# Stacking both heads of a pair on the partitions, with the odd heads' half-chunks swapped, in the state-space stage of a decoder layer

## The chip, the cores and the metric

The kernel runs on one core of one Trainium2 chip. The metric is the device time of one execution in microseconds. Everything is fp32.

## The reference

The input is x of 4 x 1024 tokens of width 256, with 16 heads of 16 channels. A layer applies three blocks, each followed by a residual addition and a layer norm: a state-space block (mamba2 with 64 states), cross-attention to 77 context tokens, and a feed-forward block with 1024 hidden units. The change concerns the first block:

```python
logA = einsum(W_logA, x) + b_logA                  # one decay per token and head
XBC  = silu(einsum(W_XBC, x) + b_XBC)              # per head: X 16, B 64, C 64
cum  = cumsum(logA over tokens)
A    = exp(cum_i - cum_j) for j <= i, else 0
G    = einsum('bihn,bjhn->bhij', C, B)
Y    = einsum('bhij,bjhc->bihc', A * G, X)
x    = layernorm(x + (gate(x) * Y) @ W_out.T + b_out)
```

## The kernel before

The 4096 tokens are cut into 16 units of 256 tokens; `stage_a`, `stage_b` and `stage_c` do the three blocks of a unit. In `stage_a` a unit has two chunks of 128 tokens (`chunk_a`), and a chunk has two half-chunks, q = 0 and 1, of L = 64 tokens. Within a half-chunk Y is computed directly through G; what comes from earlier tokens goes through a state of 64 x 16 per head, carried from one half-chunk to the next.

No scheduler reorders the work. Each step is a `part` with a name, and the tables `WHEN` and `EDGE` give each a due time in units, relative to its own unit; all parts are sorted by due time and issued in that order. The table therefore fixes the order on every engine and every queue, and lets three or four units overlap. PSUM has eight banks, handed out by one pool in that same order. All loads go through SyncE's queue, apart from the first weights, which go through ScalarE's.

The parts of the first block, with the line of their main operation:

- `pl` (L594), `cum` (L602): decay logits and their cumulative sum, written to DRAM twice by `cd` (L609) and `ce` (L614). `dl` (L622) reads `cd` back, each half-chunk's rows spread over 64 partitions; `ec` (L631) does so with `ce`, with channels on the partitions. `pcum` and `ncum` (L643, L651) give the negated sums with tokens on the partitions.
- `pb` (L674): B and C of eight heads in four banks. The rows of `bct` hold the 64 states of an even head over the 64 of an odd one. `th` (L686) and `bct` (L694) apply the silu.
- `px`, `zx`, `thx`, `xz` (L739 to L761): X with tokens on the partitions. `xz` is padded with zeros, so that the two heads of a pair write disjoint channels.
- `ex` (L798) and `sel` (L807): the decay matrix, made in place in `dl`, eight heads at a time, and its causal mask.
- `de`, `dex`, `xw` (L772 to L785): X weighted by the decay to the end of the half-chunk.
- `ptb` (L816) and `bk` (L821): B turned so that tokens are on the partitions, for four pairs at a time.
- `pg` (L834) and `st` (L845): G for each head and half-chunk on a 64x64 tile of the array, multiplied into `dl`.
- `pc`, `sn`, `pts`, `new` (L858 to L890): a half-chunk's contribution to the states, the new states with channels on the partitions (`stateT`), and those turned (`state`).
- `pyo` (L908) and `py` (L923): the output from the old states and the output within the half-chunk. `ya`, `yg`, `po_a` (L935 to L951) join them, apply the gate and project.

Before the change the rows of a tile are the 128 tokens of a chunk. A product over one half-chunk therefore runs on 64 of the 128 rows, once for each head of a pair:

```python
lhsT=xz[js, half, 4 * k + r, :],
rhs=s[f"dl{c}"][js, k, 2 * r + half, :],
start=(half == 0), stop=(half == 1),
```

In `pc` the 32 channels of a pair meet the 128 states of both heads, and half of what is made (one head's channels by the other head's states) is not used.

Of the kernel before, what the change touches and what calls it, by code (L numbers as in the profile page):

```python
# [20 lines left out]
P = 128  # L21
# [3 lines left out]
L = 64  # L25
# [12 lines left out]
    "s_c": -17.7488, "s_x": -14.3181, "s_g": -10.9930, "s_b": -8.9191, "s_x2": -8.5921,  # L38
    "keys": -6.9902, "values0": -5.1040, "s_bc": -4.2504, "s_l": -3.8501, "keys0": -3.5178,
    "load_u": -3.5043, "pl": -3.0616, "cum": -3.0081, "s_q": -2.8763, "s_z": -2.8594,  # L40
    "cd": -2.7014, "pcum": -2.4443, "ncum": -2.4136, "load_t": -2.3861, "load_u1": -2.3655,
    "dl0": -2.2598, "keys1": -2.2466, "values1": -2.2259, "px0": -2.1743, "zx0": -2.1414,
    "thx0": -1.9640, "load_k": -1.9383, "pgt": -1.9261, "px1": -1.9192, "gT": -1.8781,
    "ce": -1.8740, "zx1": -1.7566, "de0": -1.7390, "thx1": -1.5753, "ec": -1.4244,
    "ex00": -1.4225, "dex0": -1.4038, "pb0": -1.3989, "th00": -1.3867, "xz0": -1.3838,
    "bct00": -1.3681, "ex01": -1.3369, "th01": -1.3079, "load_k0": -1.3045, "dl1": -1.2878,
    "bct01": -1.2542, "sel00": -1.2073, "xw0": -1.2015, "xz1": -1.1765, "values2": -1.0810,
    "pb1": -1.0622, "de1": -1.0216, "th10": -1.0177, "bct10": -0.9976, "th11": -0.9410,
    "bct11": -0.9385, "dex1": -0.9338, "ptb00": -0.9194, "bk00": -0.8852, "ptb10": -0.8540,
    "ecx": -0.8381, "sel01": -0.8288, "values3": -0.8153, "ptb01": -0.7975, "bk01": -0.7706,  # L50
    "ex11": -0.7660, "pg0": -0.7380, "pc0": -0.7363, "bk10": -0.7222, "xb": -0.6773,
    "sn0": -0.6753, "ptb11": -0.6360, "xw1": -0.6250, "bk11": -0.6233, "st0": -0.5947,
    "sel11": -0.5768, "pts0": -0.5684, "new0": -0.5621, "s_o": -0.5243, "pc1": -0.5148,
    "py0": -0.5044, "ex10": -0.4941, "pyo0": -0.4936, "sn1": -0.4930, "ya0": -0.4577,
    "pg1": -0.4242, "sel10": -0.4139, "yg0": -0.4116, "st1": -0.3962, "pts1": -0.3944,
    "new1": -0.3793, "py1": -0.3293, "pyo1": -0.3263, "ya1": -0.2759, "poa0": -0.1943,
    "yg1": -0.1933, "r10": -0.1344, "poa1": -0.1251, "mv_a0": -0.1056, "r11": -0.0850,
    "mv_a1": -0.0791, "rs_a0": -0.0707, "ln_a0": -0.0569, "rs_a1": 0.0238, "ln_a1": 0.0482,
    "pt_b0": 0.1070, "pt_b1": 0.1865, "xT_b": 0.2141, "pq": 0.2890, "q": 0.3115, "pm1": 0.4314,
    "mx1": 0.4558, "pm0": 0.5218, "mx0": 0.5433, "s_p": 0.6203, "x1b": 0.6256, "pmt": 0.6521,  # L60
    "qm0": 0.6802, "s_1": 0.6869, "qm1": 0.7177, "pe0": 0.7713, "es01": 0.7828, "es00": 0.7874,
    "pe1": 0.8410, "s_2": 0.8624, "es11": 0.8703, "es10": 0.9335, "pa0": 0.9380, "pa1": 0.9881,
    "ot1": 1.0166, "om1": 1.0905, "ot0": 1.1466, "o1": 1.1757, "om0": 1.1997, "o0": 1.2276,
    "pob0": 1.3446, "r20": 1.4077, "pob1": 1.4668, "r21": 1.4989, "mv_b0": 1.5448,
    "mv_b1": 1.6506, "rs_b1": 1.6768, "rs_b0": 1.8518, "ln_b1": 1.8927, "ln_b0": 1.8942,
    "pt_c0": 2.2380, "pt_c1": 2.2437, "xT_c": 2.2515, "x2b": 2.2926, "ph0": 2.5349, "h0": 2.6045,
    "ph2": 2.6287, "h2": 2.6610, "ph3": 2.7023, "h3": 2.7622, "ph1": 2.8178, "h1": 2.8490,
    "pf00": 2.9287, "pf01": 3.0566, "pf10": 3.1025, "r30": 3.2254, "pf11": 3.2529, "r31": 3.2586,
    "mv_c0": 3.3511, "rs_c0": 3.6688, "ln_c0": 3.7881, "mv_c1": 3.9591, "rs_c1": 4.7458,
    "out0": 4.9977, "ln_c1": 5.5578, "out1": 6.9616,  # L70
# [4 lines left out]
        "pl": -3.6206, "cum": -3.5601, "pb0": -3.0592, "cd": -2.9747, "th00": -2.8248,  # L75
        "dl0": -2.7065, "px0": -2.6887, "pgt": -2.5368, "zx0": -2.4855, "pcum": -2.4453,
        "bct00": -2.3636, "th01": -2.2306, "gT": -2.2275, "px1": -2.1555, "zx1": -2.1167,
        "ce": -2.0684, "pb1": -2.0435, "ncum": -2.0328, "dl1": -1.9370, "thx0": -1.7699,
        "de0": -1.7454, "thx1": -1.6968, "xz0": -1.6803, "bct01": -1.6554, "ex01": -1.5524,
        "th10": -1.4592, "ec": -1.4554, "ex00": -1.4510, "ptb00": -1.4249, "sel00": -1.4027,  # L80
        "bct10": -1.3567, "bk00": -1.3010, "de1": -1.2646, "ptb10": -1.2606, "sel01": -1.1913,
        "dex0": -1.1695, "xw0": -1.1362, "th11": -1.1294, "ex11": -1.1040, "bct11": -1.0825,
        "ptb01": -1.0550, "ecx": -1.0519, "ptb11": -0.9216, "dex1": -0.8815, "xz1": -0.8643,
        "xw1": -0.8293, "bk01": -0.8006, "pc0": -0.7667, "ex10": -0.7473, "pg0": -0.7364,
        "bk10": -0.6954, "sel11": -0.6914, "sn0": -0.6792, "pts0": -0.6740, "bk11": -0.6307,
        "st0": -0.6270, "pg1": -0.6051, "new0": -0.5845, "sel10": -0.5719, "pc1": -0.5356,
        "st1": -0.5245, "pyo0": -0.5012, "sn1": -0.4950, "py0": -0.4915, "ya0": -0.4733,
        "yg0": -0.4595, "pts1": -0.4067, "xb": -0.3770, "new1": -0.3550, "py1": -0.3456,
        "pyo1": -0.3330, "ya1": -0.2992, "poa0": -0.2319, "r10": -0.2065, "yg1": -0.1630,
        "poa1": -0.1066, "mv_a0": -0.0350, "r11": -0.0322, "rs_a0": -0.0267, "mv_a1": -0.0199,  # L90
        "ln_a0": 0.0194, "rs_a1": 0.0479, "ln_a1": 0.1008, "pt_b0": 0.1064, "pt_b1": 0.1429,
        "xT_b": 0.2244, "pq": 0.2319, "q": 0.3225, "pm1": 0.4306, "mx1": 0.4701, "pm0": 0.5743,
        "mx0": 0.5866, "pmt": 0.6101, "qm0": 0.6234, "qm1": 0.6498, "pe0": 0.6979, "es00": 0.7094,
        "pe1": 0.8329, "es01": 0.8584, "es10": 0.8642, "pa0": 0.9414, "es11": 0.9582,
        "pa1": 0.9886, "ot1": 1.0223, "om1": 1.0444, "ot0": 1.1639, "om0": 1.2555, "o0": 1.2718,
        "o1": 1.2842, "x1b": 1.2969, "pob0": 1.3403, "r20": 1.4155, "mv_b0": 1.4607,
        "rs_b0": 1.4846, "pob1": 1.6460, "r21": 1.6872, "mv_b1": 1.8206, "rs_b1": 1.8604,
        "ln_b1": 1.9000, "ln_b0": 1.9037, "pt_c1": 1.9838, "pt_c0": 2.0646, "xT_c": 2.2368,
        "x2b": 2.5250, "ph0": 2.5464, "h0": 2.5900, "ph2": 2.6457, "h2": 2.6550, "ph1": 2.6766,
        "h1": 2.7411, "ph3": 2.7854, "h3": 2.8515, "pf00": 2.9091, "pf01": 3.0321, "pf10": 3.0347,  # L100
        "r30": 3.0595, "mv_c0": 3.1626, "pf11": 3.2205, "r31": 3.2894, "rs_c0": 4.4879,
        "mv_c1": 4.9536, "ln_c0": 5.6343, "rs_c1": 5.7231, "ln_c1": 6.4175, "out1": 6.9249,
        "out0": 7.0749,
    },
    1: {
        "pl": -3.0129, "pgt": -2.9113, "load_t": -2.8785, "cum": -2.6494, "cd": -2.6211,
        "pcum": -2.5596, "ncum": -2.2968, "px0": -2.2290, "dl0": -2.1919, "dl1": -1.8956,
        "zx0": -1.8203, "de0": -1.6453, "gT": -1.5667, "ex00": -1.5550, "thx0": -1.5525,
        "pb0": -1.4885, "th00": -1.4645, "xz0": -1.3885, "bct00": -1.3615, "dex0": -1.3462,
        "de1": -1.3143, "pb1": -1.2968, "th01": -1.2908, "ce": -1.2696, "load_k": -1.2501,  # L110
        "bct01": -1.2328, "px1": -1.2052, "ec": -1.1819, "zx1": -1.1474, "sel00": -1.1469,
        "xw0": -1.1209, "ex10": -1.1165, "th10": -1.1064, "ptb00": -1.0814, "ex01": -1.0691,
        "bk00": -1.0479, "ptb10": -1.0460, "bct10": -1.0155, "dex1": -1.0119, "th11": -0.9797,
        "thx1": -0.9660, "bct11": -0.8922, "sel01": -0.8844, "ex11": -0.8518, "pg0": -0.8321,
        "ptb01": -0.8265, "bk01": -0.7690, "xz1": -0.7583, "st0": -0.7572, "pc0": -0.6996,
        "sel10": -0.6991, "ecx": -0.6912, "sn0": -0.6839, "ptb11": -0.6648, "bk10": -0.6566,
        "bk11": -0.5382, "xb": -0.5286, "xw1": -0.5093, "pts0": -0.5046, "pc1": -0.4985,
        "py0": -0.4934, "sn1": -0.4909, "new0": -0.4804, "pyo0": -0.4450, "ya0": -0.4443,
        "pg1": -0.4252, "sel11": -0.4000, "pts1": -0.3929, "st1": -0.3926, "new1": -0.3821,
        "py1": -0.3595, "yg0": -0.3463, "pyo1": -0.3094, "ya1": -0.3049, "poa0": -0.2638,  # L120
# [50 lines left out]
def decoder_layer_kernel(ctx: ExitStack, tc: tile.TileContext, a: dict, out: bass.AP):  # L171
# [21 lines left out]
    def bank(shape, name):  # L193
        return ps.tile(shape, F32, tag="bank", name=name)
# [1081 lines left out]
```

## Time and profile before

| | us |
|---|---|
| median of 3 runs | 709.96 (708.72 to 715.87) |
| the profiled execution | 708.51 |
| its span, from the first to the last instruction | 706.8 |
| TensorE busy | 665.4 |
| TensorE weight loads, overlapping it | 524.1 |
| VectorE busy | 515.3 |
| ScalarE busy | 403.4 |
| GpSimd busy | 296.0 |

PE is TensorE's matmuls and PEld its weight loads; DVE is VectorE, ACT ScalarE, POOL GpSimd, and SP SyncE, which issues most transfers. The timeline gives the start and length of a burst, the engine, the line, the tiles (written <- read), and for a product the tile of the array (rows * columns) and the shape that streams through it, then the number of records. The ends of matmuls are modelled, so the printed length of a burst reaches into the next. An idle engine that is not the bottleneck costs nothing.

### The profile page before, as it was taken

The page shows a single profiled execution, that of the slowest core. Times are in us where ns is not written, and L with a number is a line of the kernel's source. Part 1 is how long each engine was busy: PE and PEld are TensorE (multiplying, and loading weights), DVE is VectorE, ACT ScalarE, POOL GpSimd, SP SyncE. Part 2 cuts the span into 40 slices and gives each one's busy share as a digit, 9 for nine tenths or more (in the row PEclk, how much of TensorE's full clock was granted, in tenths as well). Part 3 has the DMA queues.
Part 4 walks back from the last instruction along what each step waited for, and adds up shares of the span by engine and source line. Part 5 has one row for each costly group of instructions (what it writes and reads, how often), then busy time and mean ns, then how long its engine had stood idle before and what let it go on. Part 6 is the DMA issues. An engine that isn't in the chain of part 4 may idle for free.

```text
span 706.8 us, 26495 instructions
## 1 busy us (share of the span) xinstructions
PE 665.4 (94%) x11088; PEld 524.1 (74%) x11088; DVE 515.3 (73%) x1402; ACT 403.4 (57%) x1107; POOL 296.0 (42%) x525
## 2 busy tenths in 40 slices
PE   1768979999999999999999999999999999999996
PEld 0446757778878787877878787877878787777785
DVE  2636969986878778787877778686887778766643
ACT  0257768865647666575655666575666657631300
POOL 2423525544325445453444345453444435442322
PEclk9969999999999999999999999999999999999999
DMA  4543563222103022322203022222203200000001
GB/s 118 120 119 106 148 166 114 73 56 66 61 26 102 4 71 62 78 80 59 76 26 110 10 78 64 78 80 63 64 17 92 80 1 19 2 17 2 16 15 45
DMA packets 38547, 45.67 MB, mean 65 GB/s; under 512 B 10320, under 2 KB 33565, under 8 KB 38429
## 3 DMA queue, kind: packets, MB, share of 16 engines
q1 hardware_dynamic: 36960, 43.58, 21.9%
q8 instruction: 88, 1.44, 0.8%
q10 hardware_dynamic: 1468, 0.41, 0.3%
q14 instruction: 31, 0.25, 0.1%
HBM read 38.73 MB, written 5.24 MB: 62 GB/s over the span
## 4 chain that ended last, share of the span: by engine, by line
PE 90%; DMA 4%; issue 2%; DVE 1%; POOL 1%; SPq 0%; POOLq 0%; ACT 0%; ACTq 0%
PE ph L1144 16%; PE pf L1171 16%; PE pg L834 5%; PE po_a L951 5%; PE pe L1053 5%; PE pb L674 5%; PE pq L981 4%; PE pa L1078 4%; PE ptb L816 4%; PE po_b L1114 4%; PE py L923 3%; PE pm L1006 3%; DMA xu<-in_xT_dram 3%; PE pc L858 3%; PE py L908 2%; PE pts L881 2%
## 5 line engine op out<-in xcount | busy, mean ns | idle before, releaser
L798 ACT ACTIVATE dl<-dl,ncum 128x64 f32<-128x64 f32 x512 | 127.6, 337 | 0.4
L1144 PE MATMUL ph<-T_c,w 128*128 128x256 f32 x512 | 122.5, 385 | 0.0
L1171 PE MATMUL pf<-w,hT 128*128 128x256 f32 x512 | 120.8, 382 | 0.0
L807 POOL TENSOR_SCALAR_AFFINE_SELECT dl<-dl 64x512 f32<-64x512 f32 x128 | 83.9, 655 | 83.7 <-ACT dl L798 79.4
L1171 PEld LDWEIGHTS pf<-w,hT 128*128 128x128 f32 x512 | 94.2, 190 | 17.1 <-issue 5.4
L1144 PEld LDWEIGHTS ph<-T_c,w 128*128 128x128 f32 x512 | 93.8, 190 | 15.2 <-issue 2.0
L1064 ACT ACTIVATE es<-pe,mb 77x512 f32<-77x512 f32 x128 | 77.0, 680 | 46.8 <-PE pe L1053 46.8
L686 ACT ACTIVATE th<-pb 128x512 f32<-128x512 f32 x128 | 70.9, 594 | 53.4 <-PE pb L674 44.7
L694 DVE SCALAR_TENSOR_TENSOR bct<-th,pb 128x512 f32<-128x512 f32 x128 | 81.6, 679 | 8.2 <-ACT th L686 7.8
L821 ACT COPY bk<-ptb 128x512 f32<-128x512 f32 x64 | 37.2, 585 | 67.7 <-PE ptb L816 55.2
L1017 DVE TENSOR_REDUCE maxes<-pm 128x4 f32<-128x308 f32 x128 | 52.1, 470 | 9.1 <-PE pm L1006 9.1
L1160 ACT ACTIVATE hT<-ph,b 128x256 f32<-128x256 f32 x64 | 26.8, 472 | 51.8 <-PE ph L1144 36.5
L1096 POOL TENSOR_TENSOR on<-at,rec 128x256 f32<-128x256 f32 x32 | 20.2, 632 | 72.3 <-DVE rec L1091 72.3
L1155 DVE TENSOR_SCALAR hT<-ph,b 128x256 f32<-128x256 f32 x64 | 27.9, 478 | 28.0 <-PE ph L1144 28.0
L674 PE MATMUL pb<-xt,w_bc 17*64 17x256 f32 x1024 | 40.7, 396 | 4.9 <-DVE vz L506 1.8
L845 DVE TENSOR_TENSOR dl<-pg,dl 128x512 f32<-128x512 f32 x64 | 40.9, 680 | 6.1 <-PE pg L834 5.1
L548 POOL TENSOR_SCALAR rs_a<-mv_a 128x1 f32<-128x1 f32 x32 | 8.9, 277 | 75.0 <-DVE mv_a L543 73.6
L871 DVE SCALAR_TENSOR_TENSOR stateT<-stateT,ec,pc 128x128 f32<-128x128 f32 x112 | 31.8, 341 | 11.2 <-PE pc L858 9.0
L816 PE MATMUL ptb<-ident,bct 128*128 128x128 f32 x256 | 39.8, 283 | 0.0
L834 PE MATMUL pg<-bct 64*64 64x64 f32 x2048 | 38.0, 221 | 1.5 <-issue 1.4
L834 PEld LDWEIGHTS pg<-bct 64*64 64x64 f32 x2048 | 33.3, 134 | 7.7 <-issue 6.6
L951 PE MATMUL po_a<-w_out,yg 128*128 128x256 f32 x128 | 37.2, 415 | 0.0
(125 smaller groups left out, 1250.1 us busy)
## 6 DMA issues: line engine op xcount, KB each, us to landing
dl<-cd SPq DMA_DIRECT2D x64, 256.0 KB
xt<-in_xT_dram SPq DMA_DIRECT2D x64, 64.0 KB
xu<-in_xT_dram SPq DMA_DIRECT2D x16, 256.0 KB
ec<-ce SPq DMA_DIRECT2D x32, 128.0 KB
xk<-in_x_dram SPq DMA_DIRECT2D x16, 256.0 KB
out_dram<-r SPq DMA_DIRECT2D x32, 128.0 KB
w<-in_w_dram SPq DMA_DIRECT2D x2, 1024.0 KB
kv_w<-in_k_w_dram SPq DMA_DIRECT2D x1, 512.0 KB
```

What stands on the lines that cost most here:

```text
L674: nc.tensor.matmul(pbs[r][64 * half : 64 * half + 64, bc, :], lhsT=w_bc[rs, 2 * gk + half, bc, :], rhs=xt[rs, 2 * gk + half, :], start=Tru ...
L686: nc.scalar.activation(th, s[f"pb{gk}"][r], AF.Tanh)
L694: nc.vector.scalar_tensor_tensor(t, s[f"th{gk}{r}"], 1.0, s[f"pb{gk}"][r], ALU.add, ALU.mult)
L798: nc.scalar.activation(dl[:, k, h, :], dl[:, k, h, :], AF.Exp, bias=s["ncum"][:, c, 8 * k + h : 8 * k + h + 1],)
L807: nc.gpsimd.affine_select(out=d, in_=d, compare_op=ALU.is_ge, fill=0.0, base=0, pattern=[[0, 8], [1, L]], channel_multiplier=-1,)
L816: nc.tensor.transpose(v[f"ptb{k}"][:, r, :], s["bct"][4 * k + r][:, 0, cs], ident)
L834: nc.tensor.matmul(pgs[a][L * q : L * q + L, k, r, :], lhsT=t[64 * a : 64 * a + 64, 0, ts], rhs=t[64 * a : 64 * a + 64, 1, ts], start=True ...
L951: nc.tensor.matmul(v["po"], lhsT=v["yg"][:, k, :], rhs=w_out[:, k, :], start=(k == 0), stop=(k == 1),)
L1017: nc.vector.tensor_reduce(mx[:, :, at : at + 2], s[f"pm{c}"][r].rearrange("p k a s -> p a k s"), AX.X, ALU.max, negate=True,)
L1064: nc.scalar.activation(e, s[f"pe{gp}"][r], AF.Exp, bias=mb[:, b : b + 1], scale=CH**-0.5)
L1144: nc.tensor.matmul(ph[:, j, :], lhsT=w1[:, k, f * P : (f + 1) * P], rhs=s["xT"][:, k, :], start=(k == 0), stop=(k == 1),)
L1171: nc.tensor.matmul(pf, lhsT=s["hT"][:, f, c * P : (c + 1) * P], rhs=w2[:, f, :], start=(f == 0), stop=(f == FF // P - 1),)
```

## The change

The rows of a tile are no longer the 128 tokens of a chunk. For each half-chunk q the rows 0 to 63 and 64 to 127 hold the same 64 tokens for the two heads of a pair: for q = 0 the even head comes first, for q = 1 the odd head (`half ^ q` in the code). The even heads' tokens then stand in the order of the chunk, and the odd heads' half-chunks are exchanged. It follows:

- `py` is one product per pair and half-chunk over all 128 rows, and no longer two on 64 rows; so is `pc`, whose second operand is 64 wide. `stateT` is half as wide.
- `pg` makes the same products, but a bank holds one q and both row tiles of the array write to it, on different halves of its partitions.
- B is turned by halves: `ptb` makes sixteen transposes of 64 rows per chunk instead of eight of 128, into one bank per head of the pair. `bk` becomes four copies of 64 rows per chunk instead of two of 128, and has one buffer instead of two. So has `xw`, which is made in one operation on twice the elements.
- To put the tokens in place, `px`, `pts` and `pcum` are cut into products 32 columns wide. `pts` is an ordinary product with the identity now, and no transpose. `pb` writes B of the odd heads with the half-chunks exchanged, in two products of 128 columns. `xz` is written in four pieces of 64 rows instead of two of 128.
- `dl` is loaded by four transfers per chunk of half the size, instead of two. `b_l`, `w_l` and `b_x` get a second arrangement in the setup, with two more loads for `b_l` and two more for `b_x`.
- `ya` covers both half-chunks in one operation (`py` is one bank). `WHEN` and `EDGE` are replaced as a whole, so the order of all work is another. SyncE's first transfers were xu of unit 0, b_g (8 of them), cd, q_w, q_b, dl of chunk 0, xu of unit 1, ce, dl of chunk 1; they are now xu of units 0 and 1, b_g, cd, ce, cd of unit 1, dl of both chunks, xu of unit 2.

The core of the diff:

```diff
@@ dl
-                    nc.sync.dma_start(
-                        out=dl[L * q : L * q + L].rearrange("p k h i -> p (k h) i"),
-                        in_=s["cd"][2 * c + q, 0:16].partition_broadcast(L),
-                    )
+                    for half in range(2):
+                        a8 = 8 * (half ^ q)
+                        nc.sync.dma_start(
+                            out=dl[L * half : L * half + L, q],
+                            in_=s["cd"][2 * c + q, a8 : a8 + 8].partition_broadcast(L),
+                        )
@@ pb
+                for bc, half, q in ((0, 0, None), (0, 1, 0), (0, 1, 1), (1, 0, None), (1, 1, None)):
...
+                            o = o.rearrange("n (c q i) -> n q c i", c=NC, q=2)[:, 1 - q]
+                            i = i.rearrange("n (c q i) -> n q c i", c=NC, q=2)[:, q]
@@ px
-                nc.tensor.matmul(
-                    v["px"][:, :, k, :], lhsT=xus[u][:, k, cs],
-                    rhs=w_x[:, k].rearrange("x a c -> x (a c)"), start=True, stop=True,
-                )
+                for q in range(2):
+                    for m in range(4):
+                        at = c * P + L * q + 32 * (m % 2)
+                        nc.tensor.matmul(
+                            v["px"][32 * m : 32 * m + 32, q, k, :],
+                            lhsT=xus[u][:, k, at : at + 32],
+                            rhs=w_x[:, k, m // 2 ^ q, :], start=True, stop=True,
+                        )
@@ xz
+                for q in range(2):
+                    nc.vector.scalar_tensor_tensor(
+                        xz[js, q, :, half ^ q, :], thx[:, q], 1.0, zx[:, q], ALU.add, ALU.mult
+                    )
@@ xw
+            v["xw"] = tile_([P, 2, H // 2, 2 * CH], "xw", f"xw_{n}", bufs=1)
@@ ptb, bk
-                for r in range(4):
-                    nc.tensor.transpose(v[f"ptb{k}"][:, r, :], s["bct"][4 * k + r][:, 0, cs], ident)
-                v[f"bk{k}"] = tile_([P, 4, P], "bk", f"bk_{n}_{k}")
-                nc.scalar.copy(v[f"bk{k}"], v[f"ptb{k}"])
+            v["ptb"] = [bank([P, H // 2, NS], f"ptb_{n}_{a}") for a in range(2)]
+            for pair in range(H // 2):
+                for a in range(2):
+                    rs = slice(64 * a, 64 * a + 64)
+                    nc.tensor.transpose(
+                        v["ptb"][a][:, pair, :], s["bct"][pair][rs, 0, cs], ident[rs, rs]
+                    )
...
+                bk = once(v, "bk", lambda: tile_([P, 2, H // 2, NS], "bk", f"bk_{n}", bufs=1))
+                for half in range(2):
+                    js = slice(64 * half, 64 * half + 64)
+                    nc.scalar.copy(bk[js, half ^ a], v["ptb"][a][js])
@@ pg
-                                pgs[a][L * q : L * q + L, k, r, :],
+                        ns, to = slice(64 * a, 64 * a + 64), a ^ q
+                            pgs[q][64 * to : 64 * to + 64, h, :],
@@ pc
+                            v["pc"][32 * r : 32 * r + 32, q, k, :],
+                            lhsT=v["xw"][:, q, 4 * k + r, :], rhs=v["bk"][:, q, 4 * k + r, :],
@@ pts
-                    nc.tensor.transpose(
-                        v["pts"][:, q, k].rearrange("n r a c -> n (r a c)"), sn[:, q, k, :], ident
-                    )
+                    for m in range(4):
+                        nc.tensor.matmul(
+                            v["pts"][32 * m : 32 * m + 32, q, k],
+                            lhsT=sn[:, q, k, 32 * (m % 2) : 32 * (m % 2) + 32],
+                            rhs=ones[:, m // 2], start=True, stop=True,
+                        )
@@ py
-                                lhsT=xz[js, half, 4 * k + r, :],
-                                rhs=s[f"dl{c}"][js, k, 2 * r + half, :],
-                                start=(half == 0), stop=(half == 1),
+                            lhsT=xz[:, q, 4 * k + r].rearrange("p a c -> p (a c)"),
+                            rhs=s[f"dl{c}"][:, q, 4 * k + r, :], start=True, stop=True,
```

## The prediction

> **What bounds the kernel now.** I read the totals first, then a table by stage, then the chain of work that ended last, and then single stretches of the timeline.
>
> ```profile
> PE 665.4 (94%) x11088; PEld 524.1 (74%) x11088; DVE 515.3 (73%) x1402; ACT 403.4 (57%) x1107; POOL 296.0 (42%) x525
> ```
>
> TensorE (PE) is busy 94% of the span. Where are the other 6%? The table by stage (from:to, length, then the busy us of PE, weight loads, VectorE, ScalarE, GpSimd, granted clock, DMA share, GB/s):
>
> ```profile
> 0.00:20.00 20.00, 2.04 (x8) 0.95 (x12) 4.01 (x17) 1.28 (x1) 5.50 (x17) 1.00 0.42 108
> 20.00:54.00 34.00, 24.71 (x264) 16.48 (x268) 18.49 (x51) 16.11 (x52) 10.75 (x23) 0.80 0.51 125
> 54.00:74.00 20.00, 16.88 (x422) 12.67 (x412) 14.32 (x42) 15.12 (x47) 8.98 (x16) 0.91 0.41 114
> 74.00:110.00 36.00, 31.04 (x737) 23.55 (x738) 29.66 (x79) 25.77 (x71) 15.22 (x25) 0.95 0.57 153
> ...
> 200.00:300.00 100.00, 99.99 (x1681) 79.46 (x1673) 78.14 (x215) 61.63 (x166) 44.96 (x78) 1.00 0.22 60
> 300.00:400.00 100.00, 100.00 (x1799) 79.37 (x1795) 78.38 (x213) 63.90 (x181) 44.65 (x79) 1.00 0.22 63
> ```
>
> From 110 us on TensorE never stops. All its idle time lies in the first 110 us (18.0 + 9.3 + 3.1 + 5.0 = 35.4 us) and in the 5 us after its last product. So beyond the head one thing counts: TensorE's own time per unit. In the head two waits for a unit's transposed input carry the chain:
>
> ```profile
> 24.41 12.31 DMA xu<-in_xT_dram
> 38.27 10.37 DMA xu<-in_xT_dram
> ```
>
> **Prices.** In a stretch without idle, a burst costs the start of the next burst minus its own start; the printed length of a burst overlaps the next.
>
> ```profile
> 306.16 1.16 PE L834 MATMUL pg<-bct 64*64 64x64 f32 x64
> 307.25 1.22 PE L674 MATMUL pb<-xt,w_bc 17*64 17x256 f32 x32
> ...
> 310.93 0.86 PE L923 MATMUL py<-dl,xz 64*32 64x64 f32 x64
> 311.72 0.65 PE L908 MATMUL py<-bct,state 128*32 128x64 f32 x32
> 312.31 1.99 PE L1144 MATMUL ph<-T_c,w 128*128 128x256 f32 x8
> ...
> 324.25 0.41 PE L594 MATMUL pl<-xu,w_l 128*32 128x64 f32 x16
> 324.48 1.05 PE L1078 MATMUL pa<-es,vz 77*32 77x256 f32 x16
> ...
> 328.15 0.60 PE L816 MATMUL ptb<-ident,bct 128*128 128x128 f32 x4
> 328.59 0.61 PE L739 MATMUL px<-w_x,xu 128*128 128x128 f32 x4
> 329.04 1.89 PE L1171 MATMUL pf<-w,hT 128*128 128x256 f32 x8
> ```
>
> Three things are read here. (1) A transpose is one record, any other product two: ptb has 256 records for 256 transposes, px 128 for 64 products. (2) Small products on different tiles of the array run side by side: pl, 32 columns wide, is 16 records in 324.48 - 324.25 = 0.23 us, 14 ns each, where four tiles share a stream of some 57 ns. (3) A burst followed by another tile shape pays an exit: the 32 records of L908 should be 32 x 14 = 0.46 us and take 0.59 before ph, so about 0.12; by the same reckoning pg (16 steps of 58 ns = 0.93, takes 1.09) pays 0.16, py 0.14, a full 128x128 burst 0.09.
>
> **Part by part, TensorE per chunk (32 chunks).**
> ptb: eight transposes of 128 rows, 8 x 0.109 = 0.87 us, become sixteen of 64 rows, in two row tiles and two banks, with half as many moving columns. No row shows a 64x128 tile. From above: no overlap of the two row tiles, 16 x 58 ns = 0.93 us, no gain. From below: full overlap, 0.47 us. The nearest row, pg with 64-row tiles, overlaps fully, so I take 0.50: -0.37 a chunk, -11.9 us. [...]
> py: 64 records on 64-row tiles (0.79 less exit 0.14 = 0.65 us) become 32 on full rows, 32 x 14.5 = 0.47: -5.9 us.
> px, pts: full-width products of 0.45 and 0.47 us become 32 narrow records of 0.47 each: +0.8 us. pc: 0.46 to 0.47, nothing. [...] pcum: 4 records to 16: +0.9 us over 16 units. pb: 32 records to 40; a tile's stream is the same, two halves of 128 for one of 256; one step more per half tile, 0.03 us, +0.9 us.
> Sum of streams: -11.9 - 5.9 + 0.8 + 0.9 + 0.9 and +0.3 for pc = **-14.9 us**.
> Exits: px, pts, pc, py and pyo now share one shape (128 rows by 32 columns), while ptb gets a shape of its own. Counted along both programs' order of products there are 371 changes of shape before and 337 after; with the exits above 47.8 us becomes 43.8, **-4.0 us**.
> TensorE in all: -19 us. About 2.5 of 16 units do their part in the starved head, where it saves nothing: -3 back. **-16.**
>
> **The other engines, all under TensorE's cover.** ScalarE: bk turns from one copy of 128 rows into two of 64 rows; the time goes with the elements of a row (585 ns for 512), so 64 more copies, +37 us. VectorE: xz in 128 pieces instead of 64 (303 ns, same length), +19; stateT half as wide (from 341 to about 285), -6; ya joined, -9; de, -3; about zero. GpSimd: xw in one 128x512 operation at 1.27 us (the row of x1b) for two of 0.40, +16. Per 100 us ScalarE goes from 62 to about 71, VectorE stays near 80, GpSimd near 48; none is the bound. SyncE issues 64 more transfers of half the size, at 0.5 us each on a queue that has room; the bytes are the same. If bk's cover went, the whole +37 would come on top.
> **What bk's cover is.** bk and xw lose their second buffer. bk of chunk 1 waits for pc of chunk 0, and pc of chunk 1 for bk. In units 2 to 13 TensorE does between the two pc at least half a feed-forward product (1.73), pg (1.09), and pts (0.47), about 3.5 us; ScalarE needs four copies at about 0.55 from start to start and dex, 2.5 us. It fits. I take 1 us of small waits in all.
> **The head.** Every place in the order changes. xu of unit 1 is now asked for right behind that of unit 0, ahead of eight b_g transfers, so the first wait goes. But xu of unit 2 still follows ce (3.75 us of issue) and two sets of dl, and pl of unit 2 stands ahead of pb1 of unit 0 on TensorE; ptb now needs all eight bct. By that order pg of the first chunk, at 53.2 us now, comes at 50 to 54. Four more small loads (b_l, b_x) stand in ScalarE's queue, 0.7 us each, beside the wait for xu at 19.9. Bounds -8 and +8, since the two waits shown are 22 us and half the idle is spread; I take -2, as one wait goes and the next moves up little.
> Sum: 708.5 (profiled execution) - 16 + 1 - 2 = 691.5. The median shown, 709.96, lies 1.4 above that execution; I say **692**.
>
> **Rivals.**
> A. The transposes don't gain: loads bind or row tiles don't overlap. Then 12 us come back: 704. [...]
> B (slower). ScalarE comes late for bk in each chunk. The cover is 3.5 us, the chain 2.5; one group of eight exponentials of dl in between is 2.0 us (2.01 at 311.33 in ScalarE's timeline), and TensorE would wait 1.0 us a chunk: 691.5 + 32 = 724. It decides from 0.5 us a chunk. For it: one buffer, and ScalarE at 71%. Against it: nearly all of ScalarE's idle time ended with a TensorE result, so it has been early, and no exponentials stand between the pc in units 2 to 13.
> [...]
> D. The head loses the second input wait too, 10.4 us: 681.
>
> **Numbers.** Forecast (684 to 700) 0.55, A with half-gains 0.18, B 0.11, C 0.07, D 0.05, anything else 0.04. A measurement here can tell about 1%, 7 us, from no change. Faster by that: the forecast, D and a third of A, 0.66; same: the rest of A, 0.12; slower: B, C and the rest, 0.22. The range of 8 in 10 runs from 680, most of D, to 724, which takes in A and about half of B and C; the likeliest case's own is 684 to 700.
>
> **What would show it.** Right: TensorE still at 100% in the middle windows; a ptb burst of 16 in about 0.5 to 0.65 us; py in 0.47; pg still 1.09; ScalarE near 440 us busy. Wrong: a ptb burst over 0.85 (A), TensorE idle before pc ended by bk (B), pg near 2 us (C). I am wrong altogether if TensorE is not full after 110 us for another reason, such as VectorE's sn or xz late for pts and py.

## The result: no gain, and the profile after

The changed kernel takes 709.47 us (705.49 to 712.31, 20 runs), the kernel before, on the same chip, 710.93 (20 runs): a ratio of 0.9974, with a 95% interval of 0.9951 to 0.9996. The forecast was 692 us. The profiled execution of the changed kernel took 709.57 us, 1.1 more than that of before.

First the totals of the profile after:

```profile
PE 655.3 (93%) x12504; PEld 513.8 (73%) x12504; DVE 530.1 (75%) x1382; ACT 442.2 (62%) x1171; POOL 308.5 (44%) x493
```

TensorE's busy time fell by 10.1 us (665.4 before), yet the span grew from 706.8 to 707.8, so its idle time grew by 11.1. The table by stage shows where (columns as in the prediction):

```profile
0.00:20.00 20.00, 4.92 (x27) 2.58 (x28) 4.15 (x20) 0.01 (x1) 4.93 (x15) 1.00 0.39 108
20.00:54.00 34.00, 20.16 (x401) 14.58 (x394) 21.96 (x53) 16.52 (x51) 8.20 (x18) 0.85 0.39 114
54.00:74.00 20.00, 15.74 (x495) 12.08 (x492) 13.90 (x41) 14.98 (x40) 9.90 (x15) 0.83 0.35 97
74.00:110.00 36.00, 31.99 (x847) 23.42 (x849) 28.02 (x72) 34.02 (x97) 19.91 (x30) 1.00 0.58 168
...
300.00:400.00 100.00, 98.99 (x2037) 78.88 (x2028) 81.67 (x217) 69.69 (x191) 47.04 (x72) 1.00 0.21 64
```

In the head, the first 110 us, TensorE idles 15.1 + 13.8 + 4.3 + 4.0 = 37.2 us, 1.8 more than before. The rest is new: from 110 to 600 us it is busy 479.9 of 490 us, against 489.4 before. The list of TensorE's waits between 110 and 660 us (total, times, longest) held one wait of 0.6 us before and sums to 9.9 us now. Its three largest entries after:

```profile
PE py L941 <- issue: 4.4, 6, 1.0
PE py L954 <- issue: 2.0, 2, 1.7
PE pm L1035 <- issue: 1.4, 1, 1.4
```

"issue" means that the profile shows nothing the product waited for: no tile, no other engine.

Now the bursts. Two stretches of TensorE's timeline after (start, length, burst); as in the prediction, a burst costs the next start minus its own:

```profile
311.24 1.35 PE L696 MATMUL pb<-xt,w_bc 17*64 17x256 f32 x40
312.52 0.65 PE L941 MATMUL py<-bct,state 128*32 128x64 f32 x32
312.99 0.63 PE L954 MATMUL py<-dl,xz 128*32 128x64 f32 x32
...
334.89 1.22 PE L843 MATMUL ptb<-ident,bct 64*128 64x64 f32 x32
336.04 1.99 PE L1010 MATMUL pq<-T_b,q_w 128*128 128x256 f32 x8
337.97 1.16 PE L866 MATMUL pg<-bct 64*64 64x64 f32 x64
339.06 0.65 PE L887 MATMUL pc<-bk,xw 128*32 128x64 f32 x32
```

The small transposes came out as forecast: the 32 of a burst, for two chunks, cost 336.04 - 334.89 = 1.15 us, exit included. So did py, 0.47 us for 32 records, and pg still costs 1.09. But pb costs 312.52 - 311.24 = 1.28 us, where the shortest gap to the next burst before was 322.31 to 323.36, 1.05.

Last, the waits. This stretch shows what "issue" looks like in the timeline; the bracket is idle time ahead of a burst:

```profile
225.09 0.65 PE L954 MATMUL py<-dl,xz 128*32 128x64 f32 x32
225.56 0.63 PE L912 MATMUL pts<-ident,stateT 128*32 128x64 f32 x32
226.01 0.62 PE L941 MATMUL py<-bct,state 128*32 128x64 f32 x30
227.22 0.27 PE L941 MATMUL py<-bct,state 128*32 128x64 f32 x2 [0.59 <-issue]
```

The halt stands in the middle of a burst: 30 records go, and the last two, of the same tiles, come 0.59 us later. Late data is a poor reason for that. Most of these halts lie in py, pts and pm, behind some 200 to 260 records in 6 us, and each one of more than 0.6 us ends 2.2 to 2.8 us after the start of a packet on q8, the queue that the profile calls "instruction".

### The profile page after: what moved, and what is told of

Same layout as the page of the kernel before. It is cut to its first block, busy times and chain, and to the rows that moved or that the text cites. A ratio compares the mean times of both kernels' runs of the same rounds, so it can differ in the third digit from the quotient of the medians.

```text
span 707.8 us, 29317 instructions
## 1 busy us (share of the span) xinstructions
PE 655.3 (93%) x12504; PEld 513.8 (73%) x12504; DVE 530.1 (75%) x1382; ACT 442.2 (62%) x1171; POOL 308.5 (44%) x493
## 4 chain that ended last, share of the span: by engine, by line
PE 82%; ACT 6%; DMA 3%; issue 3%; DVE 2%; SPq 2%; POOL 1%; ACTq 1%; POOLq 0%; DVEq 0%
PE ph L1173 16%; PE pf L1200 16%; PE pb L696 5%; PE pe L1082 4%; PE po_b L1143 4%; PE po_a L980 4%; PE pg L866 4%; PE pa L1107 4%; PE pq L1010 3%; PE pm L1035 3%; PE py L941 2%; ACT dl L822 2%; PE py L954 2%; PE ptb L843 2%; ACT bk L854 2%
## 5 line engine op out<-in xcount | busy, mean ns | idle before, releaser
L1200 PE MATMUL pf<-w,hT 128*128 128x256 f32 x512 | 122.5, 384 | 0.0
L1173 PEld LDWEIGHTS ph<-T_c,w 128*128 128x128 f32 x512 | 93.8, 190 | 18.1 <-DVE r L988 3.4
L854 ACT COPY bk<-ptb 64x512 f32<-64x512 f32 x128 | 74.2, 579 | 42.6 <-PE ptb L843 38.7
L831 POOL TENSOR_SCALAR_AFFINE_SELECT dl<-dl 64x512 f32<-64x512 f32 x128 | 86.9, 679 | 18.8 <-ACT dl L822 13.8
L974 POOL TENSOR_TENSOR yg<-ya,gT 128x256 f32<-128x256 f32 x32 | 23.4, 730 | 134.0 <-DVE ya L969 134.0
L1125 POOL TENSOR_TENSOR on<-at,rec 128x256 f32<-128x256 f32 x32 | 19.9, 621 | 90.6 <-DVE rec L1120 87.9
L809 POOL TENSOR_TENSOR xw<-xz,de 128x512 f32<-128x512 f32 x32 | 33.6, 1048 | 33.0 <-PE pc L887 27.8
L696 PE MATMUL pb<-xt,w_bc 17*64 17x256 f32 (+1 forms) x1280 | 45.2, 354 | 1.3 <-issue 1.3
L1184 DVE TENSOR_SCALAR hT<-ph,b 128x256 f32<-128x256 f32 x64 | 27.8, 477 | 13.9 <-PE ph L1173 13.8
L696 PEld LDWEIGHTS pb<-xt,w_bc 17*64 17x64 f32 x1280 | 29.2, 135 | 12.4 <-ACT es L1093 4.4
L790 DVE SCALAR_TENSOR_TENSOR xz<-thx,zx 64x128 f32<-64x128 f32 x128 | 37.8, 333 | 0.4
```

The source lines that it names most:

```text
L696: nc.tensor.matmul(o, lhsT=w_bc[rs, 2 * gk + half, bc, :], rhs=i, start=True, stop=True)
L831: nc.gpsimd.affine_select(out=d, in_=d, compare_op=ALU.is_ge, fill=0.0, base=0, pattern=[[0, 8], [1, L]], channel_multiplier=-1,)
L854: nc.scalar.copy(bk[js, half ^ a], v["ptb"][a][js])
L1173: nc.tensor.matmul(ph[:, j, :], lhsT=w1[:, k, f * P : (f + 1) * P], rhs=s["xT"][:, k, :], start=(k == 0), stop=(k == 1),)
L1200: nc.tensor.matmul(pf, lhsT=s["hT"][:, f, c * P : (c + 1) * P], rhs=w2[:, f, :], start=(f == 0), stop=(f == FF // P - 1),)
```

## The experiments

The theory after this reading had two parts. **pb's cost is its order**: its two half products for the odd heads follow each other on the same column half of the array, and hold up the products for the other half. **The halts are instruction loads**: narrow products are issued faster than their instructions arrive. Rivals: pb pays for the number of its records; the halts are waits for bk's or xw's single buffer, or for other data, that the profile misnames. Unless stated otherwise each edit is on the changed kernel; each comparison has its own runs of the kernel before on its chip, and the ratios are to these.

**e1: pb in one product again.** The odd heads' 64-token halves are read in descending order, which exchanges them within a single product of 256 columns.

```diff
-                for bc, half, q in ((0, 0, None), (0, 1, 0), (0, 1, 1), (1, 0, None), (1, 1, None)):
+                for bc in range(2):
+                  for half in range(2):
...
+                        if bc == 0 and half == 1:
+                            o = o.rearrange("n (c q i) -> n c q i", c=NC, q=2)
+                            i = i.rearrange("n (c q i) -> n c q i", c=NC, q=2)[:, :, ::-1]
```

> The changed kernel with pb as one product again: the exchange of the odd heads' half-chunks is done by reading the 64-token pieces in descending order, so 32 records a burst and not 40. Theory (the two half products hold the in-order starts up: a burst of 40 takes 1.28 us, one of 32 took 1.05): the burst falls to about 1.05 us, 32 x 0.23 = 7.3 us of TensorE, some 6 of it beyond the head, so about 703 us beside 709.5. Rival (TensorE is no longer what sets the time, the waits grow by what it saves): 709. Rival (reading backwards costs as much): burst 1.28, 709.

Measured: 705.73 us, ratio 0.9894 (0.9857 to 0.9932). Against 0.9974 of the changed kernel that is 0.0080 x 711 = 5.7 us, and the two intervals do not touch. The burst is back at 1.05 us, and the halts are still there:

```profile
306.52 0.28 PE L941 MATMUL py<-bct,state 128*32 128x64 f32 x2
307.68 0.65 PE L941 MATMUL py<-bct,state 128*32 128x64 f32 x30 [0.88 <-issue]
...
312.64 1.12 PE L696 MATMUL pb<-xt,w_bc 17*64 17x256 f32 x32
313.69 0.65 PE L941 MATMUL py<-bct,state 128*32 128x64 f32 x32
```

**e2: the same forty records in another order.** This separates order from number.

```diff
-                for bc, half, q in ((0, 0, None), (0, 1, 0), (0, 1, 1), (1, 0, None), (1, 1, None)):
+                for bc, half, q in ((0, 0, None), (1, 1, None), (0, 1, 0), (1, 0, None), (0, 1, 1)):
```

> The changed kernel with the same 40 records of pb in another order: the two half products no longer follow each other, each stands beside a full product of the other column half. Theory (matmuls start in program order, so a half product that waits for its tile holds up what comes after it on other tiles): the burst takes about 1.08 us for 1.28, 32 x 0.2 = 6.4 us, some 5.5 beyond the head: 704. Rival (the eight more records cost 29 ns each wherever they stand): burst 1.28, 709.

Measured: 706.21 us, ratio 0.9898 (0.9861 to 0.9935), the same as e1. In its timeline pb takes 313.21 - 312.14 = 1.07 us with all 40 records:

```profile
312.14 1.14 PE L696 MATMUL pb<-xt,w_bc 17*64 17x256 f32 x40
313.21 0.65 PE L941 MATMUL py<-bct,state 128*32 128x64 f32 x32
```

So it was the order: the same 40 records take 1.28 us where the half products of one column half follow each other, and 1.07 where products for the other half stand between them. This fits the theory; which product waits for which, no run shows by itself.

**e3: pts as a transpose again.** One transpose of 128 rows per half-chunk takes the place of eight narrow products (2 records for 16), with the copies `new` by pairs of heads: four for two.

```diff
-                for k in range(2):
-                    for m in range(4):
-                        nc.tensor.matmul(
-                            v["pts"][32 * m : 32 * m + 32, q, k],
...
+                nc.tensor.transpose(
+                    v["pts"][:, q].rearrange("n r a c -> n (r a c)"),
+                    sn[:, q].rearrange("p k n -> p (k n)"), ident,
+                )
```

> The changed kernel with pts as one transpose of 128x128 per half-chunk: 2 records a chunk for 32; ScalarE then needs four copies of 128 elements for new where it had two of 256 (about 0.26 us each for 0.365). Theory (TensorE's stalls in the middle of narrow bursts, 10 us after 110 us, are instruction loads that can't keep up with narrow records at 14 ns): with 60 records fewer per unit in the run from pcum to pyo the stalls fall from 10 us to under 3, and the time by 6 to 9: about 702. Rival (pyo waits for new, made by ScalarE): new is later by 0.3 us a chunk, the stalls stay or grow: 709 to 718.

Measured: 713.68 us, ratio 0.9999 (0.9973 to 1.0026): a miss. Halts in the middle of a burst nearly went, as the theory has it, but a wait for data took their place:

```profile
PE py L950 <- ACT state L919: 8.8, 9, 1.2
```

py of line 950 reads `dl` and `xz` and no state, so what it wants from the copies is probably what they free, a bank of PSUM; this is inferred, not shown. With two copies, as the change has them, py has no such wait in the list. The narrow products thus buy a shorter hand-over, and pay for it with their number.

**e4: bk with two buffers** (`bufs=1` to `bufs=2` in the diff's bk line).

> The changed kernel with two buffers for bk, as before the change. Theory (instruction loads): the stalls stay, 709. Rival (bk of chunk 1 has to wait for pc of chunk 0, and pc, py and pyo come late): TensorE's idle time after 110 us falls from 10 us to about 1, time about 701.

Measured: 710.53 us, ratio 0.9964 (0.9946 to 0.9982), as the changed kernel; "py L941 <- issue" is still 3.7 us in five waits. The forecast's rival B falls, for bk. xw with two buffers was not tried; but between 110 and 660 us the changed kernel has no wait of TensorE for xw.

**e5: e1, and pyo of the first chunk moved behind po_b.** This breaks the narrow run at another place. `new` of the second chunk then overwrites the old states before pyo of the first reads them, so this kernel no longer computes the layer; it only times the order.

```diff
+            if name == "pyo0" and u >= 2:
+                late = max(due(u - 2, "pob0"), due(u - 2, "pob1")) - 2 + 1e-5
+                if place < late < due(u, "ya0"):
+                    place = late
```

> The kernel of e1_pb_one with one step moved: pyo of a unit's first chunk comes after po_b of the unit before last and no longer ahead of it, in most units; no instruction is added or taken away. Theory (instruction loads can't keep up with a long run of narrow records): two full-width bursts (1.8 us) now stand inside the run, in which the loads catch up, and TensorE's stalls after 110 us fall from 9.8 us to under 5: about 700 us beside 705.7. Rival (a stall belongs to the total number of records, wherever they stand): stalls 10, 706. Rival (pyo held up by its data): stalls fall too, but what is left stands at the first record of a burst.

Measured: 709.14 us, ratio 0.9946 (0.9924 to 0.9967). No gain over e1: the halts moved to pts ("PE pts L919 <- issue: 3.7, 7, 0.8"), and all waits between 110 and 660 us still come to 9.5 us. po_b stands behind the place of the halt, and pyo went behind it too; what runs ahead of it was as dense as before.

**e6: the suspected limit by itself.** The changed kernel, with 512 narrow products of pts' shape on four tiles appended, whose operands have long been in SBUF.

```diff
+        for n in range(512):
+            r = n % 4
+            nc.tensor.matmul(
+                t[32 * r : 32 * r + 32, n // 4 % 2, n // 8 % 4, :],
+                lhsT=w1[:, n // 4 % 2, 32 * r : 32 * r + 32],
+                rhs=w_out[:, n // 8 % 2, 0:L], start=True, stop=True,
+            )
```

> The changed kernel with 512 more products (1024 records, 32 columns wide, 64 streamed) at its end, on weights that lie ready, into a bank that nothing reads: the run of narrow records by itself, with no engine to wait for. Theory (instruction loads): 128 records come with each load of 16 KB, some 2.5 us from its start to use, so the run takes about 20 ns a record, 20 us, with gaps of 0.5 to 1 us in the middle of it, one per load. Rival (the array or the queue is the limit, not the loads): 14 to 14.6 ns a record throughout, 15 us, no gaps.

Measured, in the timeline of the appended part and in its table of DMA queues (packets, MB):

```profile
713.54 1.99 PE L1224 MATMUL narrow_run<-w_out,w 128*32 128x64 f32 x128 [1.75 <-issue]
717.01 1.99 PE L1224 MATMUL narrow_run<-w_out,w 128*32 128x64 f32 x128 [1.48 <-issue]
720.48 1.99 PE L1224 MATMUL narrow_run<-w_out,w 128*32 128x64 f32 x128 [1.48 <-issue]
```

```profile
q8 instruction: 7, 0.11, 1.7%
```

TensorE runs exactly 128 records in 1.99 us, stands for 1.48, and goes on, once every 3.47 us (once 3.75), with nothing else to wait for. Seven packets carry 0.11 MB, 16 KB each, about one for each block. By this count a block is one load of instructions, and in a long run a narrow record costs 3.47 / 128 = 27 ns instead of the 14 to 15 of a short burst, more than the 20 expected. This shows the limit for the appended run.

That the kernels' own halts are this limit can be counted in the traces. A record of a product comes with one of a weight load (12,504 of each in the changed kernel), so 128 records are 256 instructions. Take all instructions of TensorE in order of their start: weight loads, products and its semaphore instructions. The changed kernel has 25,212, which is 98.5 times 256, and q8 carried 98 packets; before it was 22,498, 87.9 times 256, and 88 packets. In the thirteen traces (before, after, e1 to e11) TensorE has 85 waits of 0.15 to 2.3 us put down to "issue" between 110 and 660 us. Counted round by 256, every one of the 85 stands at place 193 or 194. The appended blocks of e6 begin at 193 too, so each of these waits stands at the start of a block; waits for other engines stand at scattered places. This also answers the rival of misnamed data, for xw too: late data would not keep to one place in 256.

**e7: e1 and e3 together, with both `new` moved right behind their pts.** The second `new` then overwrites the old states before pyo of the first chunk, which waits for it; this kernel does not compute the layer either.

```diff
+            if name in ("new0", "new1"):
+                place = min(place, due(u, "pts" + name[-1]) + 1e-5)
```

> The kernel of e1_pb_one with pts as one transpose per half-chunk (as in e3_pts_transpose), and new placed right behind pts in the order, ahead of the eight exponentials that stood between them on ScalarE. Theory: the wait of pyo for new in e3 (nine of about 1.0 us) came from those exponentials and goes; with 60 records fewer in the run the instruction loads keep up as in e3; one product for pb stays: stalls under 4 us, about 697 us. Rival (four copies of new are too slow in any order): stalls of pyo for new of 0.3 to 0.6 us remain, about 703. Rival (pts as a full-width burst costs as many changes of shape as it saves): 706.

Measured: 714.26 us, ratio 1.0008 (0.9984 to 1.0032). py waits for the copies for 11.4 us in seven waits. It tells little beyond e3: the edit makes the wait that it was to remove.

**e8: the same with only the first `new` moved** (`name == "new0"`). What the expectations of e8 to e10 call the product for the decay matrix is pb.

> e1's one product for the decay matrix, plus one 128-row transpose for each half chunk of v'S-side states (pts), with the copy that y of the first chunk waits for (new0) moved right behind its own transposes. If y's wait for the copy was what took the gain away in e3, y starts without a wait, the instruction-load stalls of about 10 us shrink because two records replace eight, and the time is 697 to 703 us. Rival: the four copies and the added changes of product shape cost as much as they save, and it stays at 705 or above.

Measured: 713.11 us, ratio 1.0017 (1.0004 to 1.0029): a miss. py's wait fell to 0.7 us, and the copies were still late, for the next in line:

```profile
PE ph L1174 <- ACT state L924: 10.0, 10, 1.2
```

In ScalarE's timeline the last four copies stand behind two groups of exponentials of dl, 2.0 us each, and ph starts when they end; it reads no state either. In none of the three places tried did the transpose save more than its four copies cost, so pts stays narrow.

**e9: e1, and a full-width product put inside the narrow run.** po_b of the second chunk of unit u - 2 goes right ahead of py of unit u. Nothing else moves.

```diff
+            if name == "pob1" and 2 <= u <= 12:
+                place = min(place, 2 + due(u + 2, "py0") - 1e-5)
```

> e1's one product for the decay matrix, plus the output product of an earlier unit's second chunk (po_b, full-width matmuls of about 200 ns each) placed just before y of the first chunk, so that a full-width burst stands inside the long run of narrow products. If the stalls there are instruction loads that narrow products outrun, the stalls of 9.8 us fall under 6 us and the time to about 702 us. Rival: stalls are set by something else, stay near 10 us, and the time stays near 706 us.

Measured: 697.83 us (694.00 to 700.55), ratio 0.9792 (0.9761 to 0.9823), faster than both kernels and outside e1's interval. This is TensorE's timeline of e9 at the place where e1's, shown above, has py standing still for 0.88 us:

```profile
301.44 0.81 PE L1040 MATMUL pm<-km,q 32*128 32x154 f32 x16
302.18 1.13 PE L1148 MATMUL po_b<-p_w,o 128*128 128x256 f32 x4
303.24 0.65 PE L959 MATMUL py<-dl,xz 128*32 128x64 f32 x32
303.71 0.41 PE L917 MATMUL pts<-ident,stateT 128*32 128x64 f32 x16
303.93 0.63 PE L946 MATMUL py<-bct,state 128*32 128x64 f32 x32
304.49 0.81 PE L1040 MATMUL pm<-km,q 32*128 32x154 f32 x16
```

The same narrow products, with four records of about 0.26 us among them (303.24 - 302.18 = 1.06), and no halt. The block that ends here lasts 3.32 us in e9, without a halt, and 3.50 in e1, with the 0.88 in it; the next block lasts 5.65 us for 6.44, since the four records of po_b are no longer in it. So po_b now fills the time in which TensorE stood. In the table by stage TensorE is full again:

```profile
300.00:400.00 100.00, 100.00 (x1988) 78.25 (x1980) 84.53 (x224) 71.33 (x194) 49.84 (x78) 1.00 0.24 71
```

**e10: e9's move alone**, with pb left as the change has it: its half products stay in their order, in 40 records.

> The changed kernel with the move of e9 alone: po_b of an earlier unit's second chunk just before y of the first chunk, and the decay matrix still in five products. If the two costs are separate and add, this takes about 8 us off the changed kernel and leaves the decay matrix's 5.7 us in: 702 to 705 us, with TensorE's waits between 110 and 660 us under 6 us. Rival: e9 gained because both edits stand together, and this one alone stays near 709 us.

Measured: 706.75 us, ratio 0.9936 (0.9908 to 0.9963). It falls short of its expectation: 2.7 us below the changed kernel by the ratios, with intervals that overlap, and of 9.9 us of waits between 110 and 660 us 7.0 stay (3.5 in e9). The same move brought 0.0102 x 711.7 = 7.3 us on top of e1. The gap between these two gains is only just clear of the intervals. Seven halts at block starts stay in e10, three in e9. pb's eight more records in each burst add 32 instructions to a unit, so blocks begin at other products; whether that is the reason was not tested.

**e11: e9, with pl and cum of unit 2 behind pb1 of unit 0**, for the head.

```diff
+            if u == 2 and name in ("pl", "cum"):
+                place = due(0, "pb1") - 2 + (1e-5 if name == "pl" else 2e-5)
```

> The kernel of e9 with pl and cum of unit 2 placed right behind pb1 of unit 0, instead of ahead of it. In e9's trace TensorE waits 8.3 us at 47.6 us for xu of unit 2, with pb1 of unit 0 queued behind that wait. If this order is what keeps the head from gaining, pb1 starts between 40 and 45 us, the first pg comes at 49 to 52 us instead of 55.1, and the time falls by 2 to 4 us, to about 695 us. Rival: pb1 then waits for its banks or its silu on ScalarE instead, behind the exponentials of dl, the first pg stays after 54 us, and the time stays near 698 us.

Measured: 697.59 us, ratio 0.9809 (0.9778 to 0.9841), which can't be told from e9. In its timeline the first pg comes at 51.78 us, 3.3 earlier than e9's 55.08, so the order did hold it up. But TensorE's busy time in the first 110 us grows only from 69.0 to 71.4 us, and the measured time doesn't follow. The theory was right on the order and wrong on its worth.

## Why the prediction was wrong

Against the profiled execution of before the forecast was -17.0 us and the outcome +1.1, 18.1 apart. The gap closes with three terms: TensorE's time fell by 10.1 us where -19 was said (8.9 short), its waits after 110 us grew by 9.4 where 1 was said (8.4 short), and the head's idle time grew by 1.8, where 3 of hidden gain less 2 gives 1 (0.8 short).

The first two terms are the steps that failed: TensorE's time (pb's order, and a price for changes of shape that did not fit) and the waits.

- **What bounds the kernel: right.** TensorE's time per unit is what counts: when e9 filled it again the time fell.
- **ptb, right.** Forecast -11.9 us; the starts of all bursts, less the marked idle time, sum to -12.9 for ptb over the whole run. Rival A falls with it: the loads of 128 columns last 139 ns at the mean, but 32 transposes take 1.15 us, one every 36 ns, so the loads don't set the pace here.
- **py, right.** 0.47 us a burst as said; with the exits that it no longer pays, py within the half-chunk falls by 10.4 us.
- **pg, right.** 1.09 us as before, now with both row tiles writing to one bank, on different halves of its partitions. Rival C had pg near 2 us, the row tiles held apart on the bank they share; its chance of 0.07 rested on no run, and with the 1.09 it falls.
- **pb, the first step that failed.** "One step more per half tile, 0.03 us" counted a tile's stream and not the order in which its products are issued. Summed as for ptb, pb takes 43.0 us in the changed kernel, 37.1 in e1 and 36.6 in e2: the order costs some 6 us for the 0.9 forecast, and e1 and e2 each take it away.
- **Exits, the second.** The prediction multiplied fewer changes of shape by their old prices for -4.0 us. The parts that the change rebuilds, pb among them, came out 17.9 us lower in sum, near the 18.9 of streams and exits together. But the parts that it leaves as they were took 8.1 us more, some 5.5 of them between 110 and 690 us, where nothing was said: over the run pf +2.4, po_b +1.7, pl +1.3 and pq +1.2 are the largest, and no part fell by more than 0.6. One flaw in the price can be read: eight records of ph or pf take 1.73 us between full-width neighbours, 1.82 with a narrow burst behind them, 1.83 with one ahead and 1.92 with both (medians, before and after alike). So entering a full-width burst costs 0.10 us as well, and only leaving was in the sum. This does not explain the rest, as changes to or from a full-width shape fell too, from 224 to 197 in that stretch. No run measured this term by itself; its cause stays open.
- **Waits, the third and nearly as large as all of TensorE's shortfall.** The prediction looked at each producer (bk, xw, sn, xz) and allowed 1 us; 0.4 of the 9.9 us is for one of them (bk). It wrote that it would be wrong altogether if TensorE were not full after 110 us for another reason, and sought that reason in VectorE. The sum had narrow records at 14 to 15 ns each, which is true of a burst of 32 (0.47 us) and untrue of a long run (27 ns in e6). The changed kernel has 12,504 records for 11,088, and its new order put pts, pc, pm, py, pts and pyo side by side, where the old order had full-width po_b among them:

```profile
300.00 0.66 PE L881 MATMUL pts<-ident,stateT 128*128 128x128 f32 x4
300.49 1.03 PE L1114 MATMUL po_b<-p_w,o 128*128 128x256 f32 x4
301.83 0.92 PE L923 MATMUL py<-dl,xz 64*32 64x64 f32 x58
302.67 0.65 PE L908 MATMUL py<-bct,state 128*32 128x64 f32 x32
303.26 0.81 PE L1006 MATMUL pm<-km,q 32*128 32x154 f32 x16
```

  e6 and the count by blocks show the limit, e9 that with a full-width burst inside the run the waits between 110 and 660 us fall to 3.5 us, from 9.2 in e1. The sign was in the trace of before: four waits on "issue", 7.0 us in all, each at the start of a block of 256. Three of them lie in the head, and the longest is nearly all of this line's idle time:

```profile
L923 PE MATMUL py<-dl,xz 64*32 64x64 f32 x2048 | 29.2, 224 | 4.1 <-issue 4.1
```

- **The head, right on pg and wrong on the gain.** pg of the first chunk came at 52.9 us (50 to 54 said), and the head gained nothing (-2 said). pl of unit 2 stood ahead of pb1 of unit 0 as described; e11 shows that moving it changes pg's start and not the time.
- **The other engines, right.** ScalarE 442.2 us (about 440 said), one bk copy 579 ns, no wait on them that counts; e4 closes rival B for bk. xw took 1.05 us, not 1.27.

With pb's order and the narrow run mended, e9 gains 0.0208 x 711.7 = 14.8 us. TensorE is busy 646.7 us in it, 18.7 less than before, where -19 was said. That this meets the forecast is in part luck, since pb's smaller cost and the dearer untouched parts were not in it; but the change was worth about what was said of its streams, and was issued in an order that gave that away.

## What to carry to other kernels

Cost a stretch of small products by its record count as well as by its stream: in e6 a long run of narrow records took 3.47 us for every 128, of which 1.99 was work. A few full-width products that are due anyway can fill such time if they come before the halt (e9, 7.3 us below e1); behind it they gained nothing (e5). Products for one tile of the array should not follow each other when other tiles have work (pb: 1.28 us, and 1.07 in e2's order). If a profile shows a halt in the middle of a burst, put down to "issue", count the instructions between such halts and look at the instruction queue before looking for late data: here all 85 stood at place 193 or 194 of 256.

## What the runs showed of the hardware that was not expected

- q8 carried 98 packets of 16 KB for 25,212 instructions of TensorE, one for every 256, or 128 records with their weight loads (after); in a run without wider products such a block takes 3.47 us, of which 1.99 is work (e6). All 85 waits on "issue" in thirteen traces, between 110 and 660 us, stand at the start of such a block.
- The same 40 records of pb take 1.28 or 1.07 us, by their order alone (the changed kernel, e2).
- Between products of another tile shape, eight full-width records take 0.19 us more than among full-width ones: 1.92 for 1.73 us (before and after).
- Transposes on 64x128 tiles, the two row tiles in turn, take 1.15 us for 32 with the exit, 36 ns each (after), where those on 128x128 took 0.44 for four, 110 ns each (before), although the weight loads are as wide and last nearly as long: 139 and 146 ns at the mean.
